# Layer 0 self-attention of a decoder on one Trainium2 core: x transposed first, the second unit's maxima in the first unit's steps, the scaling of a batch's norm one step later

## The chip, the cores and the metric

The kernel runs on one core of one Trainium2 chip. The metric is the device time of one execution in microseconds; the median of several executions is compared. The engines are TensorE (PE, with its weight loads as PEld), VectorE (DVE), ScalarE (ACT), GpSimd (POOL) and SyncE (SP, which issues most DMAs).

## The reference

The reference is a decoder of two layers on 8 sequences of 512 tokens, 256 wide, in float32. Every sublayer is `x = layernorm(x + f(x))`. Only the first sublayer is touched here, the self-attention of layer 0:

```
q, k, v   = x @ W_q, x @ W_k, x @ W_v
latent    = (k + v) @ W_down_kv                    # 64 wide
k_rec     = latent @ W_up_k ;  v_rec = latent @ W_up_v
scores    = q_h . k_rec_h / sqrt(256) * exp(-0.01 |t - t'|)     # 16 heads of 16
x         = layernorm(x + softmax(scores) @ v_rec @ W_o)
```

Behind it follow cross-attention and a butterfly feed-forward net (layer 0), causal self-attention, cross-attention and a mixture of eight experts (layer 1).

## The kernel before

**Planner.** The kernel is written in a tile framework. The program text gives each instruction a place; a planner then gives each engine its order at build time, with its own estimate of when an instruction's inputs are there, and puts in the semaphores. `tc.manual_schedule(engines={PE})` keeps PE's instructions of a block in the order of the text; before the change only two stages of layer 1 use it. `tc.keep_in_program_order` pins one instruction behind what was written before it on its engine.

**Units and steps.** Layer 0's self-attention works in units `(b, g)`: batch b of 8 and a group g of four heads, 32 units. A unit has four steps, `kt` = 0 to 3, one for each block of 128 keys. The work of a unit:

- `l0_prepare(b)` (four pieces for each batch): `turn` 0 and 1 transpose x (L369, copies L370), `latent` (L377, L378), `values` (L386, L393).
- `l0_project(b, g)`: q and k of the four heads (L406, L407), copied by ACT (L408, L409).
- `l0_maxima(b, g, i)`: the scores of 128 queries (`s_sc`, L423) in two s tiles of two heads; DVE multiplies by the decay and takes each row's maximum (L428), and then `diag` (L438) keeps the block on the diagonal with the maxima taken off.
- `l0_shift(b, g)`: the maxima, negated (`mneg`, L449), are transposed (`tM`, L454) and added to q (L455); POOL makes the four products kr, kf, qf, qr (L459).
- `l0_probs(b, g, kt)`: the transposed scores (`s_st`, L472, L475; the diagonal block by transposes, L477) and ACT's exponential (`pt`, L481).
- `l0_values(b, g, kt)`: weights times values (`o_pv`, L492); `l0_finish` divides (L511 to L515).
- `l0_output(b)` (four pieces): two transposes, and two products with W_o (`o_out`, L538), to each of which DVE adds x (L541). Behind the second stands `normed(xs[b], r, on_act=True)`: statistics on DVE (L213, L214), the power on POOL (L216), `ve` on DVE (L218), and four scalings on ACT (L221).

**Order in the text.** In a step of unit n stand: the probabilities, the values of the step before, the maxima of unit n + 2 (one of its four), at `kt` 1 the shift of unit n + 1, at `kt` 2 the finish of unit n − 1, at `kt` 3 the projection of unit n + 3, at `kt` 0 and 3 one piece from the list `later` (prepare and output of the neighbouring batches), and two or three operations of the butterfly net on POOL (L299). The second product of an output mostly stands at `kt` 3 of a batch's last unit.

Ahead of the first step stands a prologue: the latent weights `wlat` (a DVE sum of two weights, L557, eight matmuls, L561, a copy, L568), the four pieces of batch 0, the projections of units 0 and 1, all eight maxima of units 0 and 1 with unit 0's shift in between, and the projection of unit 2.

**PSUM.** Three s tiles of two banks each (`s_qk`, `s_v`, `s_sc` and `s_st` all take one), one t tile (transposes, `o_lat`, `o_out`) and one o tile (`o_wlat`, `o_pv`).

Of the kernel before, what the change touches and what calls it, by code (L numbers as in the profile page):

```python
# [13 lines left out]
AF = mybir.ActivationFunctionType  # L14
ALU = mybir.AluOpType
# [3 lines left out]
P = 128  # L19
# [3 lines left out]
NT = S // P  # L23
KC = D // P
NEG = -1.0e30
LN_EPS = 1e-5
PE = mybir.EngineType.PE
# [22 lines left out]
def decoder_kernel(ctx: ExitStack, tc: tile.TileContext, a: dict, out: bass.AP):  # L50
# [12 lines left out]
    pe, act, dve, pool, sp = nc.tensor, nc.scalar, nc.vector, nc.gpsimd, nc.sync  # L63
# [31 lines left out]
    def o_tile(name):  # L95
        return pp["o"].tile([P, 512], F32, tag="o", name=name)
# [32 lines left out]
    xs = [const.tile([P, NT, D], F32, name=f"x{b}") for b in range(NB)]  # L129
# [12 lines left out]
    wkT = w0[:, 0:512].rearrange("p (c n) -> p c n", c=KC)  # L142
    wvT = w0[:, 512:1024].rearrange("p (c n) -> p c n", c=KC)
# [59 lines left out]
        transposed(xT, xs[b])  # L203
        return xT

    def normed(dst, r, on_act=False):

        st = work.tile([P, NT, 6], F32, tag="st", name="st")
        mv = work.tile([P, NT, 2], F32, tag="mv", name="mv")
        ve = work.tile([P, NT], F32, tag="ve", name="ve")  # L210
        rs = work.tile([P, NT], F32, tag="rs", name="rs")
        for i in range(NT):
            dve.bn_stats(st[:, i, :], r[:, i, :])  # L213
            dve.bn_aggr(mv[:, i, :], st[:, i, :])  # L214
        dve.tensor_scalar(ve, mv[:, :, 1], LN_EPS, None, ALU.add)
        pool.tensor_tensor(rs, ve, mhalf, ALU.pow)  # L216
        if on_act:
            dve.scalar_tensor_tensor(ve, mv[:, :, 0], -1.0, rs, ALU.mult, ALU.mult)  # L218
        for i in range(NT):
            if on_act:  # L220
                act.activation(dst[:, i, :], r[:, i, :], AF.Identity, bias=ve[:, i : i + 1], scale=rs[:, i : i + 1])  # L221
                continue
            dve.tensor_scalar(
                dst[:, i, :], r[:, i, :], mv[:, i, 0:1], rs[:, i : i + 1], ALU.subtract, ALU.mult
            )

    def r_tile():
        return work.tile([P, NT, D], F32, tag="r", name="r", bufs=1)
# [132 lines left out]
    def l0_prepare(b):  # L361


        def turn(c):
            if c == 0:
                live["xT", b] = work.tile([P, KC, S], F32, tag="xT", name="xT")
            t = t_tile("tT")
            for i in range(NT):
                pe.transpose(t[:, i, :], xs[b][:, i, c * P : (c + 1) * P], ident)  # L369
            act.copy(live["xT", b][:, c, :], t.rearrange("p i n -> p (i n)"))  # L370

        def latent():
            xT = live["xT", b]
            latT = work.tile([P, S], F32, tag="lat", name="lat")
            o = t_tile("o_lat").rearrange("p i n -> p (i n)")
            for k in range(KC):
                pe.matmul(o[0:64, :], lhsT=wlat[:, k, :], rhs=xT[:, k, :], start=(k == 0), stop=(k == KC - 1))  # L377
            act.copy(latT[0:64, :], o[0:64, :])  # L378
            live["lat", b] = latT

        def values():
            latT = live["lat", b]
            v = vaug[b % 2]
            s = s_tile("s_v")
            for t in range(NT):
                pe.matmul(  # L386
                    s[:, t // 2, (t % 2) * D : (t % 2 + 1) * D],
                    lhsT=latT[0:64, t * P : (t + 1) * P],
                    rhs=wupv,
                    start=True,  # L390
                    stop=True,
                )
            act.copy(  # L393
                v[:, :, 0:272].rearrange("p i (h n) -> p i h n", n=17)[:, :, :, 0:16],
                s.rearrange("p j (i h n) -> p (j i) h n", i=2, n=16),
            )

        return [partial(turn, 0), partial(turn, 1), latent, values]
# [123 lines left out]
    def l0_output(b):  # L522

        aT = ph.tile([P, KC, S], F32, tag="aT", name="aT", bufs=1)
        r = r_tile()

        def turn(c):
            t = t_tile("tT")
            for i in range(NT):
                pe.transpose(t[:, i, :], live["att", b][:, i, c * P : (c + 1) * P], ident)  # L530
            act.copy(aT[:, c, :], t.rearrange("p i n -> p (i n)"))

        def product(i2):
            o = t_tile("o_out").rearrange("p (j i) n -> p j (i n)", j=2)
            for j in range(2):
                i = 2 * i2 + j
                for c in range(KC):
                    pe.matmul(  # L538
                        o[:, j, :], lhsT=aT[:, c, i * P : (i + 1) * P], rhs=wo0[:, c, :], start=(c == 0), stop=(c == KC - 1)
                    )  # L540
            dve.tensor_tensor(r[:, 2 * i2 : 2 * i2 + 2, :], o, xs[b][:, 2 * i2 : 2 * i2 + 2, :], ALU.add)  # L541
            if i2 == 1:
                normed(xs[b], r, on_act=True)

        return [partial(turn, 0), partial(turn, 1), partial(product, 0), partial(product, 1)]

    with tc.tile_pool(name="bfly", bufs=1, side="right") as bfly, phase("l0_self") as ph, psum("a", 3, 1, 1):

        vaug = [ph.tile([P, NT, 288], F32, name=f"vaug{n}", bufs=1) for n in range(2)]
        mneg = ph.tile([P, NT, P], F32, name="mneg", bufs=1)  # L550
        pool.memset(mneg, 0.0)
        for n in range(2):
            pool.memset(vaug[n], 1.0)

        scored = slot("scored").rearrange("p (h n) -> p h n", h=4)
        diags = [slot(f"diag{i}").rearrange("p (i h n) -> p i h n", i=NT, h=4) for i in range(2)]
        dve.tensor_tensor(wkT, wkT, wvT, ALU.add)  # L557
        o = o_tile("o_wlat")
        for c in range(KC):
            for k in range(KC):  # L560
                pe.matmul(  # L561
                    o[:, c * 64 : (c + 1) * 64],
                    lhsT=wkT[:, k, c * P : (c + 1) * P],
                    rhs=wdown[:, k, :],
                    start=(k == 0),
                    stop=(k == KC - 1),
                )
        dve.tensor_copy(wlat.rearrange("p c n -> p (c n)"), o[:, 0 : KC * 64])  # L568
        bias_row = bfly.tile([1, 1024], F32, name="bias_row")
        sp.dma_start(out=bias_row, in_=a["ff_bexp"].rearrange("(o n) -> o n", o=1))  # L570
        butterfly = butterfly_ops(bfly, bias_row)
        units = [(b, g) for b in range(NB) for g in range(4)]
        later = []
        for piece in l0_prepare(0):
            piece()
        for u in units[:2]:
            l0_project(*u)
        for u in units[:2]:
            for i in range(NT):
                l0_maxima(*u, i)  # L580
            if u == units[0]:
                l0_shift(*u)
        l0_project(*units[2])
        for n, (b, g) in enumerate(units):
            ahead2 = units[n + 2] if n + 2 < len(units) else None
            if g == 0 and b + 1 < NB:
                later.extend(l0_prepare(b + 1))
            for kt in range(NT):
                l0_probs(b, g, kt)

                if kt:
                    l0_values(b, g, kt - 1)
                elif n:
                    l0_values(*units[n - 1], NT - 1)
                if ahead2:
                    l0_maxima(*ahead2, kt)

                if kt == 1:
                    if n + 1 < len(units):
                        l0_shift(*units[n + 1])  # L600
                elif kt == 2:
                    if n:
                        l0_finish(*units[n - 1])
                        if g == 0:
                            later.extend(l0_output(b - 1))
                else:
                    if kt and n + 3 < len(units):
                        l0_project(*units[n + 3])
                    if later:
                        later.pop(0)()  # L610
                for _ in range(3 - kt % 2):
                    next(butterfly, None)
        l0_values(*units[-1], NT - 1)
        l0_finish(*units[-1])
        later.extend(l0_output(NB - 1))
        for piece in later:
            piece()
        for _ in butterfly:
            pass
        o = o_tile("o_bias")  # L620
        for f in range(8):
            pe.matmul(o[:, f : f + 1], lhsT=bias_row[0:1, f * P : (f + 1) * P], rhs=one, start=True, stop=True)
        dve.tensor_tensor(upb, o[:, 0:8], upb, ALU.add)
# [398 lines left out]
    for c in range(4):  # L1022
        o = u_tile("o_k2")
# [582 lines left out]
```

## Time and profile before

| | us |
|---|---|
| median of 7 runs | 3594.09 (3587.44 to 3603.47) |
| profiled execution | 3591.15 |
| its span | 3589.4 |
| PE busy in the span | 3368.2 (94%) |
| DVE, ACT, POOL busy | 2081.8, 1504.2, 1096.2 |
| first maximum of unit 0 on DVE | starts at 25.45 |
| first exponential of unit 0 | starts at 58.21 |
| last exponential of layer 0's self-attention | starts at 827.21 |

The profile is of one execution. Times in its timeline count from the start of the span. A matmul's busy time is modelled and holds time in which PE waits for the next link of a chain, so the share of 94% doesn't mean that PE streams all that time. A float32 matmul shows as two records. PEclk is the clock that the throttle granted PE, as a share of the full one.

### The profile page before, as it was taken

The numbers are of one execution on the slowest core, as the hardware profiler recorded it, in microseconds if no ns is written. First come the engines' busy times: TensorE is split into PE (matmuls) and PEld (weight loads), VectorE is DVE, ScalarE is ACT, GpSimd is POOL, SyncE is SP. The second block draws the span as 40 slices with busy tenths as digits, with TensorE's granted clock in tenths as the row PEclk, the third lists the DMA queues.
The fourth block names the chain that finished last, engine by engine and source line by source line (L and its number), as shares of the span: only waits on it lengthen the run. The fifth ranks groups of instructions, "written<-read, shape, count | busy, mean of one in ns | idle before, by whom it ended". The sixth has DMA issues, their size and how long they took to land. (4 is left out here: it accounts for less than half of the span.)

```text
span 3589.4 us, 52648 instructions
## 1 busy us (share of the span) xinstructions
PE 3368.2 (94%) x19718; PEld 2120.5 (59%) x19718; DVE 2081.8 (58%) x5710; ACT 1504.2 (42%) x3139; POOL 1096.2 (31%) x960
## 2 busy tenths in 40 slices
PE   8999999998999989999999999999999998999995
PEld 3333343445666656666666665555555555888884
DVE  5776766665666467786766765666666664201012
ACT  2444444443443345565555663434433333222222
POOL 3877777781111122222222210010110111222222
PEclk8999999997999999999999999999999998999997
DMA  4101011111000089332323320000000003666674
GB/s 134 31 16 33 16 36 36 36 46 33 5 2 1 1 219 254 57 39 36 42 38 41 42 42 4 10 13 22 19 14 14 19 13 132 205 188 186 184 231 130
DMA packets 166001, 234.96 MB, mean 65 GB/s; under 512 B 26570, under 2 KB 128650, under 8 KB 165747
## 3 DMA queue, kind: packets, MB, share of 16 engines
q1 hardware_dynamic: 139010, 175.83, 15.6%
q0 software_dynamic: 25584, 51.57, 9.9%
q10 hardware_dynamic: 1152, 4.19, 0.3%
q8 instruction: 156, 2.56, 0.3%
q14 instruction: 99, 0.80, 0.1%
HBM read 135.83 MB, written 61.11 MB: 55 GB/s over the span
## 5 line engine op out<-in xcount | busy, mean ns | idle before, releaser
L428 DVE CUSTOM_DVE_ANT_0 scored<-s_sc,decay 128x512 f32<-128x512 f32 x512 | 323.5, 687 | 219.5 <-PE s_sc L423 218.4
L281 ACT ACTIVATE p<-p,nm 128x128 f32<-128x128 f32 (+3 forms) x512 | 282.5, 553 | 302.3 <-DVE nm L270 300.8
L865 POOL DMA_DIRECT2D qk<-turned x256 | 207.8, 1229 | 592.6 <-issue 303.9
L481 ACT ACTIVATE pt<-s_st 128x1024 f32<-128x1024 f32 x256 | 261.1, 1023 | 272.0 <-PE s_st L477 240.2
L1105 ACT ACTIVATE p<-s_sc,nm 128x576 f32<-128x576 f32 x256 | 191.1, 747 | 335.9 <-DVE nm L1104 236.8
L902 DVE TENSOR_SCALAR p<-p,rsum 128x576 f32<-128x576 f32 (+4 forms) x768 | 300.0, 432 | 9.8
L1462 DVE TENSOR_SCALAR y<-o_y,share 128x256 f32<-128x256 f32 x71 | 31.4, 480 | 403.2 <-PE o_y L1442 403.2
L1425 PE MATMUL s_h<-xnT,we 128*128 128x256 f32 (+1 forms) x1248 | 261.8, 363 | 1.3 <-DMA we<-in_mo_w 1.3
L270 DVE CUSTOM_DVE_ANT_0 p<-s_sc,tabs 128x128 f32<-128x128 f32 (+3 forms) x512 | 225.2, 484 | 57.0 <-PE s_sc L925 56.9
L1442 PE MATMUL o_y<-we,h 128*128 128x256 f32 x1136 | 251.4, 379 | 0.0
L1104 DVE TENSOR_REDUCE nm<-s_sc 128x1 f32<-128x576 f32 x256 | 185.4, 749 | 109.5 <-PE s_sc L1102 108.1
L1425 PEld LDWEIGHTS s_h<-xnT,we 128*128 128x128 f32 x1248 | 217.6, 192 | 26.2 <-DMA we<-in_mo_w 1.7
L1442 PEld LDWEIGHTS o_y<-we,h 128*128 128x128 f32 x1136 | 215.3, 190 | 29.0
L1463 POOL DMA_INDIRECT total<-y,to x71 | 110.1, 1551 | 399.1 <-DVE y L1462 185.7
L423 PE MATMUL s_sc<-k,q 32*128 32x512 f32 x1024 | 176.4, 678 | 25.6 <-ACT pt L481 23.2
L958 ACT COPY pt<-tP 128x384 f32<-128x384 f32 (+1 forms) x384 | 172.8, 513 | 43.6 <-PE tP L957 43.1
L925 PE MATMUL s_sc<-qk 64*128 64x128 f32 (+3 forms) x1024 | 176.4, 459 | 14.6 <-DMA qk<-turned 10.6
L1268 POOL DMA_INDIRECT rows_in<-z,irow x64 | 63.0, 984 | 403.5 <-DVE hit L1263 299.7
L1120 PE MATMUL tP<-ident,p 128*128 128x128 f32 x1024 | 144.0, 283 | 35.2 <-DVE k L1062 20.0
L957 PE MATMUL tP<-ident,p 128*128 128x128 f32 x1280 | 169.4, 276 | 5.9 <-ACT pt L958 4.6
L957 PEld LDWEIGHTS tP<-ident,p 128*128 128x128 f32 x1280 | 144.4, 141 | 50.0 <-issue 27.8
L981 PE MATMUL o_pv<-pt,vc 128*64 128x128 f32 (+1 forms) x2304 | 167.5, 290 | 0.0
(282 smaller groups left out, 6622.8 us busy)
## 6 DMA issues: line engine op xcount, KB each, us to landing
we<-in_mo_w SPq DMA_DIRECT2D x78, 1024.0 KB, 6.1
rows_in<-zero SPq DMA_DIRECT2D x64, 530.0 KB, 13.3
qk<-turned POOLq DMA_DIRECT2D x256, 128.0 KB, 4.5
coef<-in_ff_upw SPq DMA_DIRECT2D x40, 256.0 KB, 3.3
coef<-in_ff_dnw SPq DMA_DIRECT2D x40, 256.0 KB, 3.3
xr<-rows_in SPq DMA_DIRECT2D x32, 265.0 KB, 6.3
x<-in_x SPq DMA_DIRECT2D x8, 512.0 KB, 9.8
total<-x SPq DMA_DIRECT2D x8, 512.0 KB, 2.9
```

The lines of the kernel that those rows point to most:

```text
L270: dve.tensor_tensor_reduce(out=p[:, j, 0:n], in0=s[:, j, 0:n], in1=m, scale=-scale, scalar=3.0e38, op0=ALU.add, op1=ALU.min, accum_out=nm[ ...
L281: act.activation(p[:, j, 0:n], p[:, j, 0:n], AF.Exp, bias=nm[:, j : j + 1], scale=-1.0, accum_out=sums[:, at + j : at + j + 1],)
L423: pe.matmul(s[:, j, :], lhsT=q[h : h + 32, i * P : (i + 1) * P], rhs=k[h : h + 32, :], start=True, stop=True)
L428: dve.tensor_tensor_reduce(out=scored[:, h, :], in0=s[:, j, :], in1=decay[:, i, :], scale=1.0, scalar=-3.0e38, op0=ALU.mult, op1=ALU.max, ...
L481: act.activation(pt, s, AF.Exp, scale=1.0 / 16.0)
L865: pool.dma_start(out=qk[h : h + 32], in_=other[g : g + 32], accum_op=ALU.add)
L902: dve.tensor_scalar(p[:, j, 0:n], p[:, j, 0:n], rsum[:, j : j + 1], None, ALU.mult)
L957: pe.transpose(t[:, n, :], p[:, j, at * P : (at + 1) * P], ident)
L1104: dve.tensor_reduce(nm[:, j : j + 1], s, AX.X, ALU.max, negate=True)
L1105: act.activation(p[:, j, :], s, AF.Exp, bias=nm[:, j : j + 1], accum_out=sums[:, j : j + 1])
L1425: pe.matmul(s[:, j, :], lhsT=w1[:, c, f * P : (f + 1) * P], rhs=xnT[:, c, :], start=(c == 0), stop=(c == KC - 1),)
L1442: pe.matmul(o[:, i, :], lhsT=h[:, f, i * P : (i + 1) * P], rhs=w2[:, f, :], start=(f == 0), stop=(f == 7),)
```

## The change

Three things change in the text of the self-attention.

1. In the prologue, now under a manual order for PE, the two transposes of batch 0's x stand ahead of the latent weights. `latent` and the projection of unit 0 follow. `values` stands between unit 0's first and second maxima, the projection of unit 1 between the second and the third. Unit 0's shift and the projection of unit 2 end the prologue.
2. The four maxima of unit 1 leave the prologue. The steps of unit 0 now carry two maxima each: those of unit 1 in steps 0 and 1, those of unit 2 in steps 2 and 3. Unit 1's shift stands in step 2 of unit 0 instead of step 1; all later units have theirs in step 1 as before.
3. `normed` can hand its four scalings back as a closure. In `l0_output` it does: the statistics, the power and `ve` stay behind the second product, and the closure runs at `kt` 1 of the next step that has that number. That is the next unit for batches 0 to 5 (product at `kt` 3) and the same unit for batch 6 (product at `kt` 0). The last batch's follows its output directly.

```diff
+        def scaling():
+            for i in range(NT):
+                if on_act:
+                    act.activation(dst[:, i, :], r[:, i, :], AF.Identity, bias=ve[:, i : i + 1], scale=rs[:, i : i + 1])
+                    continue
...
+        if then is None:
+            scaling()
+        else:
+            then.append(scaling)
...
-                normed(xs[b], r, on_act=True)
+                normed(xs[b], r, on_act=True, then=scalings)
...
-        later = []
-        for piece in l0_prepare(0):
-            piece()
-        for u in units[:2]:
-            l0_project(*u)
-        for u in units[:2]:
+        later, scalings = [], []
+        with tc.manual_schedule(engines={PE}):
+            turn0, turn1, latent, values = l0_prepare(0)
+            turn0()
+            turn1()
+            dve.tensor_tensor(wkT, wkT, wvT, ALU.add)
...
+            dve.tensor_copy(wlat.rearrange("p c n -> p (c n)"), o[:, 0 : KC * 64])
+            latent()
+            l0_project(*units[0])
+
+            between = [values, partial(l0_project, *units[1])]
             for i in range(NT):
-                l0_maxima(*u, i)
-            if u == units[0]:
-                l0_shift(*u)
-        l0_project(*units[2])
+                l0_maxima(*units[0], i)
+                if between:
+                    between.pop(0)()
+            l0_shift(*units[0])
+            l0_project(*units[2])
         for n, (b, g) in enumerate(units):
-            ahead2 = units[n + 2] if n + 2 < len(units) else None
+
+            maxima = [(*units[n + 2], i) for i in range(NT)] if n + 2 < len(units) else []
+            if n == 0:
+                maxima = [(*units[1], i) for i in range(NT)] + maxima
+            per_step = len(maxima) // NT
+            shift_at = 1 if n else 2
...
-                if ahead2:
-                    l0_maxima(*ahead2, kt)
-
+                for _ in range(per_step):
+                    l0_maxima(*maxima.pop(0))
+
+                if kt == shift_at and n + 1 < len(units):
+                    l0_shift(*units[n + 1])
                 if kt == 1:
-                    if n + 1 < len(units):
-                        l0_shift(*units[n + 1])
+
+                    if scalings:
+                        scalings.pop(0)()
...
+        for scaling in scalings:
+            scaling()
```

More of the change, by code (lines that the diff above doesn't have):

```diff
@@ L204, in x_transposed, with normed @@
         return xT
-    def normed(dst, r, on_act=False):
+    def normed(dst, r, on_act=False, then=None):
         st = work.tile([P, NT, 6], F32, tag="st", name="st")
@@ L218, in normed @@
             dve.scalar_tensor_tensor(ve, mv[:, :, 0], -1.0, rs, ALU.mult, ALU.mult)
[L219 to L225, printed above, removed]
+        def scaling():
[3 more added lines that the diff above has]
+                    continue
+                dve.tensor_scalar(
+                    dst[:, i, :], r[:, i, :], mv[:, i, 0:1], rs[:, i : i + 1], ALU.subtract, ALU.mult
+                )
+        if then is None:
+            scaling()
+        else:
+            then.append(scaling)
     def r_tile():
@@ L556, in decoder_kernel @@
         diags = [slot(f"diag{i}").rearrange("p (i h n) -> p i h n", i=NT, h=4) for i in range(2)]
[L557 to L568, printed above, removed]
         bias_row = bfly.tile([1, 1024], F32, name="bias_row")
@@ L572, in decoder_kernel @@
         units = [(b, g) for b in range(NB) for g in range(4)]
-        later = []
-        for piece in l0_prepare(0):
-            piece()
-        for u in units[:2]:
-            l0_project(*u)
-        for u in units[:2]:
-            for i in range(NT):
-                l0_maxima(*u, i)
-            if u == units[0]:
-                l0_shift(*u)
-        l0_project(*units[2])
-        for n, (b, g) in enumerate(units):
-            ahead2 = units[n + 2] if n + 2 < len(units) else None
+        later, scalings = [], []
[4 more added lines that the diff above has]
+            dve.tensor_tensor(wkT, wkT, wvT, ALU.add)
+            o = o_tile("o_wlat")
+            for c in range(KC):
+                for k in range(KC):
+                    pe.matmul(
+                        o[:, c * 64 : (c + 1) * 64],
+                        lhsT=wkT[:, k, c * P : (c + 1) * P],
+                        rhs=wdown[:, k, :],
+                        start=(k == 0),
+                        stop=(k == KC - 1),
+                    )
+            dve.tensor_copy(wlat.rearrange("p c n -> p (c n)"), o[:, 0 : KC * 64])
+            latent()
+            l0_project(*units[0])
+            between = [values, partial(l0_project, *units[1])]
+            for i in range(NT):
+                l0_maxima(*units[0], i)
[3 more added lines that the diff above has]
+            l0_project(*units[2])
+        for n, (b, g) in enumerate(units):
+            maxima = [(*units[n + 2], i) for i in range(NT)] if n + 2 < len(units) else []
[3 more added lines that the diff above has]
+            shift_at = 1 if n else 2
             if g == 0 and b + 1 < NB:
```

## The prediction

> **What bounds the kernel now.** I read the page first, then the windows, the list of waits up to 850 us, and the timeline. All parts of the change lie before 850 us; behind that the order of work is the same, so a shift there moves the end one for one.
>
> ```profile
> PE 3368.2 (94%) x19718; PEld 2120.5 (59%) x19718; DVE 2081.8 (58%) x5710; ACT 1504.2 (42%) x3139; POOL 1096.2 (31%) x960
> ```
>
> TensorE is the bound by this line, but its share is modelled. The windows (columns: busy PE, PEld, DVE, ACT, POOL; PEclk; DMA) show where it only waits:
>
> ```profile
> 25.00:30.00 5.00, 3.95 (x16) 0.90 (x12) 4.37 (x12) 0.56 (x1) 2.65 (x3) 0.89 1.05 390
> 30.00:35.00 5.00, 4.68 (x14) 1.67 (x14) 4.79 (x16) 0.00 (x0) 0.72 (x1) 0.50 0.92 265
> 50.00:55.00 5.00, 5.00 (x8) 1.46 (x8) 4.79 (x15) 0.00 (x0) 0.00 (x0) 0.50 0.00 0
> 60.00:65.00 5.00, 5.00 (x47) 2.23 (x45) 3.24 (x10) 2.79 (x4) 0.00 (x0) 1.00 0.00 0
> 250.00:255.00 5.00, 3.17 (x12) 1.33 (x12) 1.04 (x3) 3.16 (x6) 3.67 (x3) 0.57 0.19 47
> ```
>
> Up to 55 us VectorE is full (the maxima of units 0 and 1), ACT is empty, and PE holds half its clock. From 60 us, in the steps, it is the other way round. At 250 us the clock has dropped again. The waits up to 760 us say why:
>
> ```profile
> ACT x L221 <- DVE ve L218: 30.0, 6, 5.0
> PE s_sc L423 <- ACT pt L481: 23.2, 6, 3.9
> ```
>
> Six times ACT stands 5.0 us at the scaling of a norm, and six times PE then stands 3.9 us. The timeline there:
>
> ```profile
> 228.62 0.75 DVE L213 BATCH_NORM_STATS2 st<-r 128x6 f32<-128x256 f32 x2
> ...
> 242.45 1.99 PE L538 MATMUL o_out<-wo,aT 128*128 128x256 f32 x8
> 243.08 0.69 ACT L409 ACTIVATE k<-s_qk,aug 128x512 f32<-128x512 f32 x1
> 245.23 0.66 PE L477 MATMUL s_st<-ident,diag 128*128 128x128 f32 x4
> 248.80 2.08 ACT L221 ACTIVATE x<-r,ve,rs 128x256 f32<-128x256 f32 x4 [5.02 <-DVE ve L218]
> 250.78 1.91 ACT L481 ACTIVATE pt<-s_st 128x1024 f32<-128x1024 f32 x2
> ```
>
> The exponentials had their scores at 245.8 and ran at 250.8, behind the scaling. And of the prologue and one step:
>
> ```profile
> 25.45 0.69 DVE L428 CUSTOM_DVE_ANT_0 scored<-s_sc,decay 128x512 f32<-128x512 f32 x1 [12.26 <-PE s_sc L423]
> 45.44 0.48 PE L369 MATMUL tT<-ident,x 128*128 128x128 f32 x1
> 58.21 1.94 ACT L481 ACTIVATE pt<-s_st 128x1024 f32<-128x1024 f32 x2
> 68.28 1.16 PE L423 MATMUL s_sc<-k,q 32*128 32x512 f32 x8
> 69.45 0.69 DVE L428 CUSTOM_DVE_ANT_0 scored<-s_sc,decay 128x512 f32<-128x512 f32 x1 [1.24 <-PE s_sc L423]
> 70.82 0.91 PE L472 MATMUL s_st<-qr,kf 32*128 32x384 f32 x4 [0.39 <-DVE mx L428]
> 72.20 1.03 ACT L481 ACTIVATE pt<-s_st 128x1024 f32<-128x1024 f32 x1 [2.73 <-PE s_st L477]
> ```
>
> A step is a ring: scores, two VectorE passes that free an s tile, s_st, exponential, next scores. Only three s tiles exist.
>
> **Part 1, the prologue.** x is transposed ahead of the latent weights. Its landing isn't shown: it is issued 1.05 us before wvT, which had landed at 6.44; the loads of wkT and wvT behind it are 0.5 MB, 1.7 us at the some 300 GB/s that the queue then moved, so 4.7 (an estimate). Transposes take 8.73 to 11.80 before, 3.07; then wlat 1.97 and its copy 0.34: the latent can start at 10.1, not 12.47, −2.4 (−0.7 if x lands with wvT). Values (16.42 to 18.34, 1.92) and the second projection (21.31 to 24.27) leave the path; only k's copy stays, to 22.59 before. From the latent to the first maxima: 3.32 + 0.63 + 3.03 + 1.26 + 1.18 = 9.4, so VectorE starts at 19.5 instead of 25.45. Its four maxima take 13.6 (3.40 each, 31.42 to 34.82), plus 0.6 because the second projection (3.0 at full clock) stands among them, longer than the VectorE work queued in the tiles: 33.7. Then maximum, transpose, sum: 1.3 to PE's release at 35.0 (q follows on VectorE; Pool's two products, 2 × 1.26, end near 38.4 and free the q tile before the projection needs it). Projection of unit 2 at half clock 5.1 (51.79 to 56.9), and 1.33 from the first s_st to the first exponential: 41.4 instead of 58.21. That is −16.8; −14.7 if the first projection runs at half clock too (5.1 for 3.0).
>
> **Part 2, four more maxima in unit 0's steps.** Here the gain is handed back. A step without projection takes 4.97 (67.23 to 72.20). With tiles A (s_st), B and C (two maxima), from B's scores at 0: VectorE starts at 1.17 and frees B's tiles at 2.5 and 3.7; diag to 4.5; C's tiles free at 5.9 and 7.1. The next A has the tiles of B's second and C's first, so it completes at 5.9 + 0.84, its exponential starts 0.54 later at 7.3, and the next scores 1.04 later: 8.35, +3.4. That is the whole price of a maxima (3.40): VectorE's idle before the next scores (1.2 in the row at 69.45) is not filled, because the next B needs that exponential's tile. Likewise I get +4.0 for the first step (3.98 before) and +2.5 for the last (7.23, where the projection already covers a part): 3.4 + 3.4 + 4.0 + 2.5 = 13.3. diag measures 0.69 while Pool is idle and 1.28 in the mean of the stage; a stretch of 0.59 in each of the four extra is 2.4, I take half: 1.2. The shift of unit 1 one step later costs nothing: its products need some 5 us and the next unit is a step and a half away; uncovered, that is 5. Bounds: VectorE alone would allow 2 × 3.40 a step, 4 × (6.8 − 4.97) = 7.3.
>
> The clock: maxima with PE at 1.2 of 3.4 us hold 0.50 (30 to 55 us); steps with 4.6 of 4.97 hold 1.00. A double step has 5.8 of 8.35, 0.70, between 0.35 and 0.92 and a little nearer the second. At half clock the end of a step (s_st, transposes, o_pv: 0.91 + 0.66 + 1.06) doubles, +2.6; four steps: 0 to 10.5. I take a quarter, 2.6. [...]
>
> Parts 1 and 2: −16.8 + 13.3 + 1.2 + 2.6 = +0.3. Bounds: −16.8 + 7.3 = −9.5 below, −14.7 + 13.3 + 2.4 + 10.5 = +11.5 above.
>
> **Part 3, the scaling.** Nothing is added: 4 ACT instructions a batch, 2.08, no DMA, no queue but ACT's (SP's and Pool's order is kept). The closure moves them in the program, behind the exponentials of the next unit's steps 0 and 1. But ACT isn't under the manual order, and the trace shows that the order on the chip is not the program's: the statistics at 228.62 belong to the norm written behind the product at 242.45, three steps later; at 846.80 ACT copies weights written after the last scaling, which follows at 849.05. Work goes out when the planner believes it ready. In its picture the scaling was ready before the exponentials, otherwise these, idle ACT before them, would have gone first already. The chip says 248.8 against 245.8; the planner prices PE dearer: of four equally ready transposes of x1 it slipped one (45.44) into PE's prologue, which on the chip was mostly waiting. Its picture at a norm is not touched by this change, so I expect the scaling in the old place: 0. If an exponential now slips between the four, up to three of them (1.5 us) a norm are saved, 7 × 1.5 = −10 at most; nearest row is the unbroken x4, so 0.
>
> **Sum.** The profiled execution took 3591.15 (span 3589.4 and 1.75 around it), 2.9 under the median of 3594.09. 3591.15 + 0.3 = 3591.45; on the median's footing 3594.4.
>
> **Rivals.**
> *The scaling does move (faster).* From the last exponential before a norm to step 2 behind it: 238.40 to 263.66 = 25.26; without a norm 73.41 to 91.02 = 17.61, with the same PE pieces within 0.1 (1.99 + 0.66 against 0.66 + 1.93). The excess is 7.65, for later batches 8.0 (643.28 to 669.05 = 25.77 is 8.2). Six of them 48, the seventh (ACT idle 3.71) about 4: 52. The 2.08 fit into ACT's 2.73 idle at step 1. VectorE's wait for Pool in the chain stays (1.15 and a stretched ve of 1.23), some 1.4 each, 10: −42, so 3552 (3542 to 3560). For: it is what the text says. Against: the hoisted rows.
> *Half clock through unit 0 (slower).* PE's waits in double steps (0.6 and 1.3) drop the clock all along, with the slow first projection and diag stretched: +11.5, so 3606. Without the clock these come to +1.0, so it decides (past +7.2) from three fifths of the four steps at half clock, a PEclk of 0.7 there.
> *VectorE hides more than the ring lets me think:* −9.5, so 3585. Against: the planner would have to reorder s tiles.
> *Nothing of part 3 happens* is my forecast itself.
>
> **Numbers.** A measurement of this kernel can tell about 0.2%, 7.2 us. Forecast 0.46 (own range 3586 to 3602), scaling moved 0.30, half clock 0.19, overlap 0.05: faster 0.35, same 0.46, slower 0.19. The range runs from 3550, inside the moved case (some 0.12 left out below), to 3606 (0.06 above).
>
> **What would show it.** Right: first scored near 19.5, first exponential near 41 to 44, scored-to-scored in unit 0 near 8.4 a step, unit 1's first exponential at 77 to 83 (79.43 before), L221 still ahead of the exponentials with 5 us of ACT idle. Wrong: L221 behind the exponentials of step 1, no drop of the clock near 250 us, and the stage 40 us shorter; or PEclk 0.5 to 0.7 from 45 to 80 us.

## The result, and the profile after

| | before | after |
|---|---|---|
| median of the runs compared | 3597.83 us (64 runs) | 3586.9 us (25 runs) |
| ratio | | 0.9973, interval 0.9964 to 0.9982 |
| profiled execution, its span | 3591.15, 3589.4 | 3593.76, 3592.0 |
| last exponential of the stage starts at | 827.21 | 816.02 |

The changed kernel is faster by 0.27%, some 10 us. I had forecast no change (+0.3 us). Its median of 3586.9 lies just inside the 3586 to 3602 that I gave, but against 64 runs of the kernel before the gain is clear of the noise. The two profiled executions show the opposite sign, although the stage ends 11.2 us earlier: behind its last exponential, where the text is the same, one took 2762.2 us and the other 2776.0. Later traces with the same text there give 2762.8 to 2778.3, so a span cannot carry a difference of 10 us. I read the stage by its own times and the whole by medians. (Medians below stand beside runs of the kernel before on the same chip: 3597.27 for the first four experiments, 3600.66 for the next four, 3597.01 for the last three.)

The page, and the waits up to 760 us, of the changed kernel (its lines stand further down: L221 is now L223, L423 is L430, L481 is L488):

```profile
PE 3359.8 (94%) x19718; PEld 2122.0 (59%) x19718; DVE 2083.7 (58%) x5710; ACT 1503.2 (42%) x3139; POOL 1095.6 (31%) x960
```

```profile
ACT x L223 <- DVE ve L218: 30.0, 6, 5.0
PE s_sc L430 <- ACT pt L488: 17.3, 6, 2.9
```

ACT's wait at the norm is what it was, six times 5.0. Only TensorE's wait for the exponential behind it is shorter, 2.9 instead of 3.9. ACT's timeline at the second batch says why:

```profile
246.41 0.69 ACT L416 ACTIVATE k<-s_qk,aug 128x512 f32<-128x512 f32 x1
252.12 1.09 ACT L223 ACTIVATE x<-r,ve,rs 128x256 f32<-128x256 f32 x2 [5.02 <-DVE ve L218]
253.12 1.91 ACT L488 ACTIVATE pt<-s_st 128x1024 f32<-128x1024 f32 x2
254.93 0.58 ACT L508 COPY oT<-o_pv 128x512 f32<-128x512 f32 x1
255.39 1.10 ACT L223 ACTIVATE x<-r,ve,rs 128x256 f32<-128x256 f32 x2
```

The x4 has become two x2. In the text all four stand behind the exponentials of two steps; on the engine the planner put two ahead of step 0's exponentials and two behind. The first of them still holds ACT until the norm's statistics are there, but what runs between that wait and the exponentials is 1.0 us instead of 2.0.

The start and the first unit, from the timeline (the first row is of the kernel before, the others of the changed one):

```profile
9.19 0.29 DVE L568 COPY w<-o_wlat 128x128 f32<-128x128 f32 x1 [2.06 <-PE o_wlat L561]
```

```profile
11.07 0.55 DVE L164 TENSOR_SCALAR w<-w,noaug,aug 128x512 f32<-128x512 f32 x1 [3.59 <-DMA w<-in_decay]
...
13.53 0.55 DVE L164 TENSOR_SCALAR w<-w,noaug,aug 128x512 f32<-128x512 f32 x1
13.99 0.28 DVE L584 COPY w<-o_wlat 128x128 f32<-128x128 f32 x1
...
14.42 3.32 PE L384 MATMUL o_lat<-xT,w 128*64 128x512 f32 x4 [4.95 <-DVE w L584]
...
23.14 0.69 DVE L435 CUSTOM_DVE_ANT_0 scored<-s_sc,decay 128x512 f32<-128x512 f32 x1 [8.87 <-PE s_sc L430]
...
46.54 1.94 ACT L488 ACTIVATE pt<-s_st 128x1024 f32<-128x1024 f32 x2
53.92 1.02 ACT L488 ACTIVATE pt<-s_st 128x1024 f32<-128x1024 f32 x1 [2.39 <-PE s_st L484]
```

The first exponential comes 11.7 us earlier than before (58.21), and unit 1's at 84.00, 4.6 later than before (79.43): unit 0 with its eight maxima takes 37.46 instead of 21.22. The windows (columns as before) show the clock in it, and at the norm:

```profile
60.00:65.00 5.00, 4.03 (x28) 1.78 (x28) 4.03 (x10) 1.02 (x1) 1.27 (x1) 0.66 0.00 0
70.00:75.00 5.00, 4.15 (x22) 1.58 (x24) 3.25 (x10) 1.33 (x2) 2.27 (x2) 0.69 0.01 3
250.00:255.00 5.00, 2.09 (x10) 0.80 (x8) 2.45 (x5) 2.88 (x5) 5.00 (x5) 0.78 0.00 2
```

In two of the double steps the mean clock of a 5 us window is about two thirds (0.66 and 0.69); the dip at the norm is still there (0.78 here, and 0.54 in the window behind it).

### The profile page after: what moved, and what is told of

It reads as the page before. It is cut to its first block, busy times and chain, and to the rows that moved or that the text cites. A ratio compares the mean times of both kernels' runs of the same rounds, so it can differ in the third digit from the quotient of the medians.

```text
span 3592.0 us, 52645 instructions
## 1 busy us (share of the span) xinstructions
PE 3359.8 (94%) x19718; PEld 2122.0 (59%) x19718; DVE 2083.7 (58%) x5710; ACT 1503.2 (42%) x3139; POOL 1095.6 (31%) x960
## 5 line engine op out<-in xcount | busy, mean ns | idle before, releaser
L488 ACT ACTIVATE pt<-s_st 128x1024 f32<-128x1024 f32 x256 | 260.9, 1023 | 273.4 <-PE s_st L484 244.0
L946 PE MATMUL s_sc<-qk 64*128 64x128 f32 (+3 forms) x1024 | 176.8, 461 | 13.3 <-DMA qk<-turned 9.9
L430 PE MATMUL s_sc<-k,q 32*128 32x512 f32 x1024 | 163.9, 649 | 21.1 <-ACT pt L488 17.3
```

Of the source, the lines that this page charges most:

```text
L488: act.activation(pt, s, AF.Exp, scale=1.0 / 16.0)
```

## The experiments

For the comparison inside the stage I use unit lengths: from the second exponential of a unit's step 0 to that of the next unit. N is the sum of the six units in whose last step a norm is made for the next (7, 11, 15, 19, 23, 27), F that of the six behind them, 30 the unit of batch 6's norm, U0 the first unit; the "13 unit lengths" of some expectations are N, F and 30 together. Each is from one trace. Traces differ: in the three with the old start (before, 2 and 6), whose engines run the same instructions in the same order up to there, unit 1's first exponential comes at 79.43, 84.59 and 82.45; in those of the new start (changed, 1 and 4) at 84.00, 84.58 and 84.51.

| kernel | median, us | ratio (interval) | N | F | 30 | U0 |
|---|---|---|---|---|---|---|
| before | | 1 | 179.9 | 147.9 | 18.8 | 21.5 |
| changed | 3586.9 | 0.9973 (0.9964 to 0.9982) | 173.3 | 143.5 | 15.3 | 37.8 |
| 1 start and maxima only | 3598.97 | 1.0006 (0.9987 to 1.0026) | 179.9 | 147.5 | 16.3 | 39.7 |
| 2 scaling only | 3587.21 | 0.9976 (0.9962 to 0.999) | 173.3 | 144.1 | 15.3 | 24.3 |
| 3 wlat's copy on ACT | 3588.36 | 0.9972 (0.9958 to 0.9987) | 173.3 | 144.2 | 18.4 | 40.6 |
| 4 scaling pinned | 3560.89 | 0.9891 (0.9871 to 0.991) | 153.9 | 138.9 | 13.4 | 39.7 |
| 5 unit 1's maxima back | 3587.41 | 0.996 (0.9945 to 0.9974) | 173.3 | 144.5 | 18.4 | 21.6 |
| 6 old start, pinned | 3560.26 | 0.9886 (0.9867 to 0.9905) | 153.9 | 138.8 | 13.4 | 21.5 |
| 7 as 3, values in the gap | 3588.14 | 0.9964 (0.9952 to 0.9977) | 173.3 | 144.3 | 18.4 | 37.8 |
| 8 as 7, pinned | 3557.46 | 0.9877 (0.9858 to 0.9896) | 151.9 | 138.5 | 13.4 | 40.6 |
| 9 as 5, pinned | 3555.66 | 0.9877 (0.9858 to 0.9897) | 154.1 | 138.9 | 13.4 | 21.6 |
| 10 as 5 and 7, pinned | 3553.56 | 0.9862 (0.9841 to 0.9883) | 149.6 | 136.9 | 13.4 | 21.6 |
| 11 as 4, GpSimd quiet | 3921.44 (one run) | | 143.8 | 133.2 | 13.4 | 37.4 |

**1. The start and the maxima alone.**

```diff
-                normed(xs[b], r, on_act=True, then=scalings)
+                normed(xs[b], r, on_act=True)
```

> The changed kernel with the scalings put back straight behind the statistics, as before; the new prologue alone. Theory A (the prologue and the four fuller steps of unit 0 lose, the gain comes from the scalings): second exponential of unit 1's step 0 at 85.2 as in the changed kernel (80.6 before), and from there the lengths of before, so the last exponential of the stage at 827.2 + 4.6 = 831.8; time about 4 us above the kernel before, near +0.1%. Theory B (the gain comes from the prologue): last exponential near 816, time 10 us below the kernel before.

Measured 1.0006, with N as before to 0.1 us. Parts 1 and 2 together are worth nothing that the medians show, as my sum of +0.3 had it; the interval leaves room for 5 us less and 9 more. The last exponential came at 824.61, not at theory A's 831.8: unit 6 took 22.16 instead of 28.59 and unit 30 took 16.3 instead of 18.8, though neither has another text (on unit 6 see experiment 11). ACT's timeline has the old row again, unbroken:

```profile
249.13 2.07 ACT L223 ACTIVATE x<-r,ve,rs 128x256 f32<-128x256 f32 x4 [5.02 <-DVE ve L218]
```

**2. The scaling alone**: the kernel before with the closure, run at `kt` 1, and nothing else.

> The kernel before with the scalings handed back as a closure and run in step 1; the old prologue. Theory A: the scalings stand split in two and two around the exponentials, ACT still waits 5.0 us for the norm; each norm unit 1.0 to 1.7 us shorter, the one of batch 6 3.5, together -15.8: last exponential at 811.4, time -16 us or -0.44% against the kernel before. Theory B: last exponential at 827, time as before.

Measured 0.9976, 10 us below the kernel before, with N 173.3 as in the changed kernel and the same two and two on ACT. By the medians the gain is this part's. The expected −16 us and last exponential at 811.4 were missed (it came at 818.38): the same start as before ran later in this trace, with unit 1 at 84.59.

**3. The queue in front of the latent.** wlat's copy on VectorE stands behind three decay-table operations that wait for a DMA. Here ACT makes it.

```diff
-            dve.tensor_copy(wlat.rearrange("p c n -> p (c n)"), o[:, 0 : KC * 64])
+            act.copy(wlat.rearrange("p c n -> p (c n)"), o[:, 0 : KC * 64])
```

> The changed kernel with the copy of the latent weights (L584) moved from DVE to ACT, nothing else. Theory A: the copy stood on DVE behind the decay tables that wait for their DMA (9.5 to 13.99); on ACT it runs at about 9.5 and the latent starts at 10 instead of 14.4; first scored 4.3 us earlier, near 18.8, and the first exponential near 42.3 instead of 46.5; last exponential 811.7, -4.3 against the changed kernel. Rival: something else is as late (a weight, the decay table), then the first exponential moves by less than 1.

The queue was what held the latent: it starts at 10.13, 4.3 earlier. The expectation for what follows was missed: the first exponential comes at 49.37, later than in the changed kernel (46.54). The clock is at half from 20 us, and again from 45 to 50, where the changed kernel had 1.00 in both windows:

```profile
20.00:25.00 5.00, 4.74 (x16) 2.50 (x8) 3.22 (x9) 0.17 (x1) 1.60 (x2) 0.50 1.10 354
45.00:50.00 5.00, 5.00 (x17) 2.04 (x18) 0.00 (x0) 1.80 (x3) 5.00 (x5) 0.50 0.00 0
```

**4. The scaling held where the text has it.**

```diff
-                    act.activation(dst[:, i, :], r[:, i, :], AF.Identity, bias=ve[:, i : i + 1], scale=rs[:, i : i + 1])
+                    ins = act.activation(dst[:, i, :], r[:, i, :], AF.Identity, bias=ve[:, i : i + 1], scale=rs[:, i : i + 1])
+                    if then is not None:
+                        tc.keep_in_program_order(ins)
```

> The changed kernel with each deferred scaling pinned behind what was written ahead of it on ACT, so that the four really come behind the exponentials of step 1. Theory A (ACT's queue holds the exponentials back): no wait of ACT for the norm, no PE wait of 3 us and no drop of the clock near 250; units with a norm 5 to 6 us shorter, 27.7 to about 22.5, their followers about 1 shorter: last exponential at 778 to 788, time about 1% below the kernel before (3555 to 3565). Rival C (DVE's own wait for the power on POOL, 1.15, and the stretched ve of 1.23 ahead of the next maxima hold the step as much): units shorten by 2 at most, last exponential near 803, time -0.6%.

Measured 0.9891: 1.09%, some 36 to 39 us below the kernel before, and 26 below the changed kernel. Its timeline and window at the same norm (its lines stand two further down than in the changed kernel):

```profile
246.02 1.02 ACT L490 ACTIVATE pt<-s_st 128x1024 f32<-128x1024 f32 x1 [1.99 <-PE s_st L486]
...
253.82 2.06 ACT L223 ACTIVATE x<-r,ve,rs 128x256 f32<-128x256 f32 x4
```

```profile
250.00:255.00 5.00, 4.70 (x40) 2.14 (x40) 4.31 (x10) 3.12 (x5) 4.40 (x4) 1.00 0.14 43
```

The exponential no longer stands behind the norm, the scalings follow those of step 1 without a wait, and the dip of the clock is gone. Neither of the two waits is in the list of waits any more. Four, two and no scalings ahead of the exponentials give N of 179.9, 173.3 and 153.9: the first two are worth 1.1 us a norm, the last two with the wait another 3.2 (5 to 6 were expected). The last exponential, at 786.92, and the median lie in theory A's ranges; rival C's 803 and −0.6% are out.

**5. Unit 1's maxima back ahead of the first exponential**, with the rest of the changed kernel.

```diff
+            for i in range(NT):
+                l0_maxima(*units[1], i)
             l0_shift(*units[0])
...
-            if n == 0:
-                maxima = [(*units[1], i) for i in range(NT)] + maxima
...
-            shift_at = 1 if n else 2
+            shift_at = 1
```

> The changed kernel with the second unit's four maxima put back ahead of the first exponential; everything else stays. Theory (a pass of maxima costs the ring of scores the same wherever it stands): the first exponential comes 13 to 16 us later than the changed kernel's 46.54, at 60 to 62; unit 0 falls back from 37.46 us to 21 to 25; the second unit's first exponential stays within 3 us of 84.00, and the median within 0.15% of the changed kernel's 3586.9. Rival (the move into unit 0's steps is what gave the 4.6 us away, because the half clock stretches the long steps): the second unit's first exponential comes at 77 to 80 and the median 4 to 7 us below the changed kernel.

In its trace the first exponential comes at 56.56 and unit 1's at 77.86:

```profile
56.56 1.94 ACT L488 ACTIVATE pt<-s_st 128x1024 f32<-128x1024 f32 x2
...
77.86 1.02 ACT L488 ACTIVATE pt<-s_st 128x1024 f32<-128x1024 f32 x1 [0.18 <-PE s_st L484]
```

Against the changed kernel's trace, putting them back costs 10.0 us at the start and saves 16.2 in unit 0; unit 1 comes 6.1 earlier, the rival's number. In the start, part of the four maxima hides other work. In the changed kernel the transposes of unit 0's shift wait for VectorE's last maxima; here they run while VectorE still has the last of unit 1's maxima to do (first row of the changed kernel, then two of this one):

```profile
39.30 1.12 PE L461 MATMUL tM<-ident,mneg 128*128 128x128 f32 x4 [5.41 <-DVE mneg L456]
```

```profile
49.36 1.11 PE L461 MATMUL tM<-ident,mneg 128*128 128x128 f32 x4
...
52.44 0.68 DVE L445 TENSOR_TENSOR diag<-scored,mx 128x512 f32<-128x512 f32 x1
```

So TensorE's transposes come 10.1 us later for 13.6 us of maxima. From the transposes to the first exponential both traces take 7.2 us, so the half clock of unit 2's projection in the changed kernel (0.54 from 40 to 45 us) is not where the difference lies. How much of the 6.1 lasts is open: experiment 9 has the same start, and its trace has the first exponential at 61.15 and unit 1's at 82.45, inside the theory's ranges and not the rival's. Unit 1 came earlier than in the changed kernel both times, by 6.1 and 1.6. The median, 0.996 against 0.9973, points the same way but within the intervals.

**6. The old start with the scaling pinned.**

> The kernel before, with the four scalings handed on to the step after and kept in program order there; its start is the old one. Theory (the start is worth nothing that lasts, all the gain is in the scaling): the 13 unit lengths sum to 305 to 312 us, as in the pinned changed kernel (306.1), and the median is 3555 to 3565 beside its 3560.9. Rival (the new start is worth about the 11.7 us by which its first exponential is earlier, and something hides it): 3569 to 3575.

Measured 3560.26, N, F and 30 as in experiment 4. The medians show no worth of the new start here either; the rival's 3569 to 3575 is out.

**7. The value product in TensorE's wait for k's copy**, on top of experiment 3.

```diff
             l0_project(*units[0])
+            values()
-            between = [values, partial(l0_project, *units[1])]
+            between = [partial(l0_project, *units[1])]
```

> The kernel with wlat's copy on ScalarE, and with the value product (eight matmuls, 1.99 us) put ahead of the first maxima, into the 1.26 us in which TensorE waits for k's copy. Theory (in the kernel with the copy on ScalarE alone the granted clock fell to 0.50 at 19.4 us, after that gap, and the half clock took the 4.3 us of earlier start): with the gap filled the clock holds at 1.00 from 20 to 30 us, the first scores come at about 20.5 and the first exponential at 42 to 44. Rival (the half clock comes whatever fills that gap, by what the steady matmuls before it drew): 0.50 from about 20 us again and the first exponential at 48 to 50. In both the median stays between 3582 and 3592, since the start is a few us of it.

The first exponential comes at 43.89, inside the theory's 42 to 44, but the clock holds only to 25 us (0.99 from 20 to 25, 0.50 from 25 to 30). That the gap of 1.26 us triggers the drop is not shown, and experiments 5 and 9 tell against it: in both TensorE waits for k's copy at about 21 us (1.26 up to 21.84 in 5's trace; in 9's, with the same text, TensorE is busy 3.74 of the 5 us from 20 to 25), and only in 9 does the clock drop there (0.80 from 20 to 25 us, then 0.50; 1.00 in both windows in 5).

**8. The same start, pinned.**

> The same start as the run with the value product in the gap, with the scalings kept in program order behind the two exponentials of step 1. By the theory (start and scaling are separate) the 13 unit lengths sum to 304 to 312 us and the median is 3555 to 3562; if the start's earlier first exponential lasts, up to 4 us less than the pinned changed kernel's 3560.9. Rival (what the start gains is given back in the first units): within 2 us of 3560.9.

3557.46, inside the theory's 3555 to 3562 (the 13 unit lengths sum to 303.8, just below its 304); its interval covers experiment 4's ratio, so what its start is worth stays open.

**9. Unit 1's maxima back, pinned.**

> The changed kernel's transposes-first start, the second unit's maxima back ahead of the first exponential, and the scalings kept in program order behind step 1's exponentials. Theory (the three parts add: -1.6 for the start, +6.1 avoided, -40.5 for a scaling that really moves): second unit's first exponential at 77 to 80, 13 unit lengths 304 to 309 us, median 3553 to 3559 where the pinned changed kernel had 3560.9. Rival (what the first units gain is lost in the later stages' spread or to a stall in unit 6): within 2 us of 3560.9 or above.

3555.66, as expected, but unit 1's first exponential is at 82.45, not 77 to 80. The start is that of experiment 5, line for line in the text, and yet the clock differs. The window from 25 to 30 us, first of experiment 5, then of this one:

```profile
25.00:30.00 5.00, 3.94 (x14) 1.28 (x14) 3.97 (x12) 1.01 (x1) 0.00 (x0) 1.00 1.06 382
```

```profile
25.00:30.00 5.00, 3.84 (x12) 2.56 (x15) 2.88 (x9) 1.01 (x1) 0.28 (x1) 0.50 1.05 379
```

Two executions of the same start lie 4.6 us apart in the first exponential (56.56 and 61.15); those of experiments 7 and 8 lie 3.8 apart in unit 1's (81.37 and 85.15). That is as much as experiment 3 or 7 was to show, so the clock's part in their times is an observation of one execution each, and their medians, 0.9972 and 0.9964, don't separate them from the changed kernel.

**10. All of it: copy on ACT, values in the gap, unit 1's maxima back, scaling pinned.**

> The same with wlat's copy on ScalarE and the value product ahead of the first maxima. Theory (the work comes 2.6 us earlier, but the half clock comes earlier too): second unit's first exponential 75 to 79 and the median within 2 us of the run with the copy on VectorE. Rival (the half clock comes after a fixed stretch of dense matmuls, so that an earlier start is lost whole): 79 to 82, and the median 1 to 3 us above it.

3553.56, ratio 0.9862: the lowest median here, 1.4% below the kernel before. Unit 1's first exponential is at 74.41, earlier than either range. That speaks against the rival, but it is one execution, and two of one start differed by 4.6. Against experiment 9 the 2.1 us are within the intervals.

**11. GpSimd quiet.** Units 6 and 15 vary by up to 6.6 us between traces of kernels that don't differ there. In the changed kernel's trace, unit 6 (27.31; 22.16 in experiment 1's) has this on VectorE and GpSimd:

```profile
194.10 9.25 DVE L445 TENSOR_TENSOR diag<-scored,mx 128x512 f32<-128x512 f32 x1
194.22 2.46 POOL L306 TENSOR_TENSOR wup<-wup,coef 128x512 f32<-128x512 f32 x2
...
201.54 1.25 POOL L466 TENSOR_TENSOR kf<-k,w 128x512 f32<-128x512 f32 x1
```

A subtraction of 0.69 us takes 9.25 here, until 0.55 us behind the last of GpSimd's products, which follow each other without a pause to 202.79. In experiment 1's trace the same subtraction, at the same place of the same queue of products (from 186.95 to 205.55), took 2.06:

```profile
196.25 2.06 DVE L445 TENSOR_TENSOR diag<-scored,mx 128x512 f32<-128x512 f32 x1
```

In all traces here unit 6 takes 27.3 to 28.8 where it holds such a diag of 9.2 to 9.3, and 22.2 where it doesn't. The edit to experiment 4's kernel takes the butterfly's products out of the steps; they are done behind the last unit.

```diff
-                for _ in range(3 - kt % 2):
-                    next(butterfly, None)
```

> The pinned changed kernel with the butterfly's products taken out of layer 0's steps on GpSimd and done after the last unit; the same is computed. Theory (a subtraction on VectorE that starts while GpSimd has products queued back to back is held until they end): no diag above 3.5 us (with the products in the steps, 9.25 at 194.10 in the changed kernel and up to 9.39 in the pinned one), the busy time of the 128 diags falls from 163 us to 90 to 115, and unit 15 gets shorter by 4 to 7 us; the total is longer, since several hundred us of products on GpSimd follow the stage. Rival (the long diags come of something else, such as the mean of TensorE's scores): diags of 9 us remain and the busy time stays above 150 us.

VectorE's groups up to 850 us, of experiment 4 and then of this one (behind the bar: busy us, mean ns of one):

```profile
L447 DVE TENSOR_TENSOR diag<-scored,mx 128x512 f32<-128x512 f32 x128 | 163.3, 1276 | 2.4
```

```profile
L447 DVE TENSOR_TENSOR diag<-scored,mx 128x512 f32<-128x512 f32 x128 | 117.9, 921 | 2.4
```

The longest diag is now 1.72 us, unit 15 falls from 31.12 to 23.97 (7.2, just over the 4 to 7 expected), and N and F together by 15.8. The busy time, 117.9, stays a little above the 90 to 115 expected (a diag takes 0.69 in the median, 0.92 in the mean); the shift's own products are still on GpSimd in the steps, but whether these diags meet them is not shown. The whole takes 3921.44, longer as expected, since the products follow the stage. So the long diags come of GpSimd's products, and the rival falls. The theory's rule, that a diag is held until the queue ends, does not hold: in the changed kernel's trace 61 diags start in an unbroken row of products (gaps under 0.1 us) with more than 3 us of it left, and two are held to its end (194.10 and 419.25); the other 59 take 3.3 us or less. What decides is not shown.

## Why the prediction was wrong, point by point

**Part 3 is the step that failed.** Its term was 0, "nearest row is the unbroken x4, so 0". It measured −14.5 in the units concerned (N −6.6, F −4.4, unit 30 −3.5; the last two also shift by 1 and 3 us between traces with the same scaling), and 0.24% as a median, some 9 to 10 us, in experiment 2. I had the mechanism of the smaller gain in the text (an exponential slipping between the four, "up to three of them (1.5 us) a norm", −10 at most) and set it to nothing. Two slipped, 1.0 us each norm on TensorE's wait, 1.1 in the unit; the −10 had no term for the units behind a norm. The step went wrong by treating the planner as all or nothing: the old row, four ready operations in one block, was taken for evidence of where they would stand when the text puts them elsewhere. That the planner hoists them was right, in part; why it hoists just two isn't shown.

**The rival of a scaling that moves** was priced rightly: −42 against −40.5 in the 13 units of experiment 4 and 36 to 39 as a median. It had its chance of 0.30 for a condition that the change doesn't meet; one pin meets it.

**Part 1** gave −11.7 at the first exponential for −16.8 forecast. x landed at 4.98 us (4.7 assumed) and the transposes were done at 7.87. The step that failed is "the latent can start at 10.1": I priced TensorE's chain and left out VectorE's queue, on which wlat's copy (0.28 us) stood behind the decay tables and their DMA. In the trace of before the copy ran ahead of them, at 9.19; the planner changed VectorE's order too. The latent started at 14.42; experiment 3 puts it at 10.13. Of the 5.1 missed, 4.3 are this, −0.7 a shorter way to the first maxima (8.7 for 9.4), and 1.5 lie behind them.

**Part 2** was right in size: 16.2 more in unit 0 for the 17.1 of 13.3 + 1.2 + 2.6. Exponential to exponential, the middle steps took 8.81 (53.92 to 62.73) and 9.68 for 8.4 forecast, with the clock between 0.66 and 1.00. Where it was at 0.50 (62 to 65 us), the end of a step did take nearly twice as long as in the trace of before: 1.12 for 0.66 (transposes, at 61.94) and 1.94 for 1.06 (o_pv, at 62.98). The mean clock over unit 0 is 0.91, and 0.87 in experiment 1's trace; if the rest was at 0.50, that is 18% and 26% of the time (an estimate), near the quarter that I took for it. The ring held: TensorE waits for VectorE's maxima up to 1.48 us in such a step. VectorE overlapping more, and half clock all through unit 0, are both out for this kernel.

**Parts 1 and 2 together** gave +4.6 in the two traces, for +0.3. Part of that is the trace of before, the earliest of the three with the old start: the means of three and three traces (82.16 and 84.36) are 2.2 apart. The medians of experiment 1 show 0.06%, so the sum stands within what can be told. What I missed is that the same maxima are partly hidden where they stood: 10.1 us at the start for 13.6 us of work, against 16.2 in the steps (experiment 5).

Of the signs named, L221 ahead of the exponentials with 5 us of idle ACT came true in half, since two of four had gone behind. First scored (23.14 for 19.5), first exponential (46.54 for 41 to 44) and unit 1's (84.00 for 77 to 83) were all late by the queue in part 1.

## What to carry to other kernels

A planner that orders an engine by readiness doesn't take a moved line of text as an order: look at the engine's timeline after the change, and pin the instruction if the place is what matters (here the change as written was worth 10 us and the pin another 26). Price a start on every engine in the chain, with what stands in each queue ahead of the one small copy. Work that is moved behind a boundary has to be priced with what it overlapped in the old place, not only with its own length. Before a difference between two traces is explained, look at how far two traces of the same code lie apart.

## What the runs showed of the hardware

**GpSimd's queue can hold VectorE.** A two-tensor subtraction that takes 0.69 us when no GpSimd product overlaps it took up to 9.39 among products queued without a gap (experiment 4); in the traces of before and after, two each took 9.25 to 9.36 and ended 0.55 us behind the last of them. Those of before start at 189.50 (9.26) and 419.19 (9.35), and I had priced diag by its mean of 1.28. It is rare: two of the 62 such starts in the trace of before, and two of the 61 in that of after. The 9.25 us at 194.10 span seven products of some 1.25 each, and with the butterfly's products out of the steps the longest diag was 1.72 (experiment 11).

**The clock of the same start differed between two executions**: 1.00 and 0.50 from 25 to 30 us in experiments 5 and 9. What decides is not shown. Their first exponentials, at 56.56 and 61.15, lie 4.6 us apart, so I take it (an estimate from these two) that one execution tells nothing below some 5 us about a start here.
